# A Macaron block with 4-bit weights: the second wave's even planes on ScalarE, the first results' splits put off, ScalarE's casts at the ends of waves, and the opening's loads reordered

## The chip, the core and the metric

The kernel runs on one core of a Trainium2 chip. The core has a matrix engine (PE, TensorE), three engines for elementwise work (DVE is VectorE, ACT is ScalarE, POOL is GpSimd) and a sequencer that mostly issues transfers (SP). Each engine works through its own queue in order and waits at semaphores for the others. The metric is the device time of one execution in microseconds (us), as the median of several runs. The profile comes from one further execution, which has a time of its own.

## What is computed

The input is x of 2 x 1024 tokens with 1024 features. Three blocks follow each other, each on a layer-normalised copy of its input:

```
x = x + 0.5 * ffn(layernorm(x))
x = x + s4(layernorm(x))              # a convolution along the features
x = x + 0.5 * ffn(layernorm(x))
ffn(x) = (silu(x @ Wg) * (x @ Wu)) @ Wd
W[k, n] = s[k // 128, n] * (q4[k, n] - (z4[k // 128, n] + 1))
```

Wg and Wu are 1024 x 2752, Wd is 2752 x 1024. They come as 4-bit numbers, eight to a 32-bit word (the eight are eight consecutive rows k), with a scale and a zero point for each group of 128 rows. Both ffn blocks use the same weights.

## The kernel before

**Jobs.** The 2048 tokens are cut into four blocks of 512. Four blocks times two ffn passes make eight jobs, j = 0 to 7. Each job has an *up* stage (`gate_up`: the products with Wg and Wu, silu and the product of the two) and a *down* stage (`down`: the product with Wd). The change touches job 0 only, which is also the job in which the packed weights are first unpacked.

**The up stage.** The 43 column units (128 columns each of Wg or Wu, the last one shared by two half units) are taken in eight waves: waves 0 to 4 have six units (three of Wg, three of Wu), waves 5 and 6 have four, wave 7 has five. A wave holds one PSUM bank per unit and goes through the eight groups of 128 rows, g = 0 to 7. One wave and one g make a *step*: s = 8 * wave + g, 64 steps in all. In a step PE multiplies each unit's weights twice, once with the high part of the tokens (`xTh`, fp32r) and once with the low part (`xTl`, fp16), so a step of six units is twelve matmuls of line L842. After a unit's second matmul the bank is rescaled in place by the ratio of two groups' scales: even units by ACT (L800), odd ones mostly by DVE (L804), and PE may go on adding to that bank only afterwards. At g = 7 ACT makes the silu (L874) and DVE the product hf (L877) (`gated`), and POOL splits hf into a high and a low half for the down stage (hh, L879, and hl, L881).

**How a weight gets to PE.** For wave w:

- `fetch(w)` loads the packed words (L558) and `fetch_zeros(w)` the zero points (L565, from a table that the kernel wrote to DRAM itself).
- `split(w)` runs six DVE operations over them (`signed_bytes`): shift and mask for the even and for the odd nibbles (L619, x2), then for each of the two an addition of the zero points (L623) and an exclusive or that makes the byte a signed one (L625).
- `dequantize(w, j)`, j = 0 to 7, copies one of eight byte planes to int8 rows (L659, on POOL). Even j come from the even nibbles, odd j from the odd ones.
- `keep_bytes(w, odd)` writes the four even or the four odd planes to the DRAM tensor `wq` of the wave (L665, issued by SP).
- `load_bytes` reads 128 rows of `wq` for one step (`b<-wq`, L761, SP), and `make_weights` casts them to fp32r (`w_up`): on ACT (L775) where j = 0 and s > 2 and s % 8 is 1, 2 or 5, on POOL otherwise (L777). `next_weights` at step s loads for step s + 4 and casts for step s + 3. All of a step's rows hold even and odd planes, so none can be read before both writes have landed.

Wave 0 goes a shorter way in `start()`: `first_split` makes its bytes, with the even planes on ACT (L602, an addition of -128 on bytes that are still unsigned) and the odd ones on POOL (L600), each followed by a small transfer `b<-q` (L603, SP) of the first step's rows straight to the first byte tile. `keep_first` writes the rest to DRAM (L607). The layer norm of the first token block also runs there: `first_moments`, `first_rows` (normalised rows, L1793 on ACT, L1795 on DVE), and `first_turn(c)`, which transposes one block of 128 features on PE (L1808) and splits it into `xTh` and `xTl`: with ACT (L1810) and DVE (L1811), or for c = 3 and 5 with a copy by ACT (L1814) and the split on POOL (L1815, L1816). Block c is used from g = c on.

**What sets the order.** The program is written step by step; `at(up, s, f)` hangs a piece of other work before the products of step s, or at s + 0.5 between its two halves. `first_weights` gives the steps at which the splits, copies and writes of each wave are hung. A planner then orders each engine's instructions: by the order of writing among those that it holds to be ready, so that a later instruction can overtake an earlier one that it takes to be waiting. Where a piece is wrapped in `in_order_of_writing` or `pinned`, its instructions on the named engines keep the order of writing. DVE's splits and SP's loads are pinned in that way, and so is all of `start()`. The copies of L659, the casts on POOL and the splits of hf are not.

**Buffers.** hf has three buffers (`hfpool`), the cast weights five, the byte tiles six.

Of the kernel before, what the change touches and what calls it, by code (L numbers as in the profile page):

```python
# [32 lines left out]
GK = 8  # L33
# [24 lines left out]
def macaron_s4_kernel(  # L58
# [495 lines left out]
    def fetch(w, queues=(nc.sync, nc.sync)):  # L554

        raw = t4(f"raw_{w}").bitcast(I32)[:, : width_of(w)]
        for own, i, lo, hi in columns(w):
            queues[i].dma_start(raw[:, own], (gate_qw, up_qw)[i][:, lo:hi])  # L558
        packed[w] = [raw, None]
# [51 lines left out]
    def signed_bytes(key, raw, even, z):  # L611
# [9 lines left out]
        for part in (even, raw):  # L621
# [3 lines left out]
            nc.vector.tensor_scalar(both, both, 0x8080, None, ALU.bitwise_xor)  # L625
            yield

    def split(w):
        raw, z = packed[w]
        even = t4(f"even_{w}").bitcast(I32)[:, : width_of(w)]  # L630
        return signed_bytes(w, raw, even, z)
# [21 lines left out]
    def dequantize(w, j):  # L653
# [5 lines left out]
        nc.gpsimd.tensor_copy(unpacked[w][:, j % 2, j // 2, :], packed[w][j % 2][:, j // 2, :])  # L659
# [45 lines left out]
    def first_weights(up, dn, at):  # L705
# [3 lines left out]
        for w in range(1, len(WAVES)):  # L709
            s0 = (0, 4, 8 * w - 15)[min(w, 3) - 1]  # L710
            steps = (0.5, 1, 2, 2.5, 3, 3.5) if w == 1 else range(6)
            in_pieces(at, [(up, s0 + d) for d in steps], lambda w=w: split(w))
            copies = {1: (3.5,) * 8, 2: (3, 3, 4, 4, 6, 6, 7, 7)}.get(w, (3, 3, 4, 5, 6, 6, 7, 8))
# [5 lines left out]
            for odd, o in enumerate({1: (3.5, 3.5), 2: (5.5, 7.5)}.get(w, (6.5, 9.5))):  # L719
# [12 lines left out]
        for n in range(6 * 8):  # L732
            k, j = divmod(n, 8)
            a, rt = divmod(k, 3)
            if j == 0:
                at(*when(max(0, n - 7)), lambda a=a, rt=rt: fetch_down(a, rt))
                steps = [when(max(0, n - d)) for d in (4, 3, 3, 2, 1, 0)]
                if n == 16:
# [31 lines left out]
    def make_weights(i):  # L770
# [3 lines left out]
        if j == 0 and stage == "up" and s > 2 and s % GK in (1, 2, 5):  # L774
# [31 lines left out]
    def gate_up(j, b, hooks):  # L806
        hi, lo = pieces[b]
        ps = {}
        for s, (wi, g) in enumerate(STEPS):
            if j == 0 and s < 8:  # L810
# [61 lines left out]
    def gated(j, f, pg, pu):  # L872
# [6 lines left out]
        nc.gpsimd.tensor_copy(hi, hf)  # L879
        lo = hpool.tile([P, TB], F32R, tag="h", name=f"hl_{j}_{f}")  # L880
        nc.gpsimd.tensor_tensor(lo, hf, hi.bitcast(F32), ALU.subtract)  # L881
        h[f] = (hi, lo)

# [691 lines left out]
    def fast():  # L1575
# [5 lines left out]
        for j, (b, k) in enumerate(JOBS):  # L1581
# [88 lines left out]
            if j == 0:  # L1670
# [11 lines left out]
                steps = [(up, s) for s in range(17, 35, 2)]  # L1682
# [4 lines left out]
                for t in (0, 2):  # L1687
                    more = lambda t=t: first_rows(t, 512, HID)
                    at(up, 1, pinned(more, ET.DVE))
# [107 lines left out]
    def first_turn(c):  # L1797
# [11 lines left out]
        if c not in (3, 5):  # L1809
# [14 lines left out]
    def start():  # L1824
# [12 lines left out]
        for j in (1, 3):  # L1837
            dequantize_first(j)
        fetch(1)
        for j in (5, 7):  # L1840
            dequantize_first(j)
        first_scales = scales_in_pieces(0, 3, srow)
        mv, scratch = first_moments()
        next(first_scales)
        for j in (0, 2):
            dequantize_first(j)
# [5 lines left out]
        dequantize_first(4)  # L1852
# [115 lines left out]
```

## Time and profile before

| | |
|---|---|
| median of three runs | 2046.01 us (2045.63 to 2046.46) |
| the profiled execution's own time | 2046.72 us |
| its span, first to last instruction | 2044.9 us |
| PE busy | 2008.3 us (98%) |
| first matmul of L842 | 19.75 us |
| job 0's up stage, from there to the first matmul of L927 | 178.2 us |
| matmuls in it | 688 |
| a step of twelve matmuls with nothing in its way | 2.70 us |

Times within the trace are counted from the first instruction. A row of the timeline gives the start, the duration, the engine, the line, what is written and read with its shape, and how many like instructions were merged; the bracket gives the engine's idle time before it and what ended that. In a row that ends with "<-DMA b<-wq", the engine had nothing to do until that transfer had landed. A row of the windows gives the busy time of each engine within a stretch, then the mean TensorE clock (PEclk, 1.00 is full speed), the share of the transfer engines and GB/s. A busy PE can be a slow PE: the clock column tells.

### The profile page before, as it was taken

How to read it: one execution, taken by the hardware profiler on the slowest of the kernel's cores; microseconds unless marked ns; L12 is line 12 of the kernel's file. 1: busy time of each engine (PE TensorE's matmuls, PEld its weight loads, DVE VectorE, ACT ScalarE, POOL GpSimd, SP SyncE). 2: the span in 40 equal slices, each digit the busy share in tenths (PEclk: the TensorE clock that was granted, in tenths of full speed). 3: DMA queues.
4: the chain of work that ended last, by engine and by line, in shares of the span. 5: the costliest groups of instructions: out<-in, count | busy, mean ns of one | idle time of the engine just before them, and what ended most of it. 6: DMA issues, size and time to landing. Idle time of an engine off the chain costs nothing.

```text
span 2044.9 us, 29679 instructions
## 1 busy us (share of the span) xinstructions
PE 2008.3 (98%) x9202; PEld 1374.2 (67%) x9202; DVE 1628.9 (80%) x2712; ACT 1413.8 (69%) x2218; POOL 1369.2 (67%) x1772
## 2 busy tenths in 40 slices
PE   6999999999999999999999999999999999999998
PEld 4555776577766678665876578667686676866576
DVE  7887878867888787877778777887878878777776
ACT  6788787747675476777767777664776647767775
POOL 5877768757875478755976568754686636965542
PEclk9999999999999999999999999999999999999999
DMA  4334332233623327411462126333163331661113
GB/s 144 117 100 143 112 89 78 66 76 98 165 79 84 91 52 195 136 32 35 124 182 81 31 51 162 90 87 87 43 157 102 76 89 43 157 192 36 34 36 102
DMA packets 345965, 197.13 MB, mean 96 GB/s; under 512 B 166989, under 2 KB 323670, under 8 KB 345798
## 3 DMA queue, kind: packets, MB, share of 16 engines
q1 hardware_dynamic: 344382, 192.74, 34.7%
q10 hardware_dynamic: 1288, 2.01, 0.3%
q8 instruction: 75, 1.23, 0.2%
q14 instruction: 92, 0.75, 0.1%
q0 software_dynamic: 128, 0.39, 0.1%
HBM read 127.52 MB, written 48.57 MB: 86 GB/s over the span
## 4 chain that ended last, share of the span: by engine, by line
PE 91%; DVE 3%; POOL 2%; issue 1%; DMA 1%; ACT 1%; SPq 0%; DVEq 0%; POOLq 0%; ACTq 0%
PE pg L842 56%; PE po L927 30%; PE pc L1295 3%; PE pb L1295 1%; POOL q L659 1%; DVE pg L804 1%; DMA wq<-q 1%; ACT pg L800 0%; POOL w_up L777 0%; DVE po L804 0%; DVE rawd L623 0%; POOL hl L881 0%; DVE hf L877 0%; DVE rawd L619 0%; DMA b<-wq 0%
## 5 line engine op out<-in xcount | busy, mean ns | idle before, releaser
L800 ACT ACTIVATE pg<-pg,rat 128x512 f32<-128x512 f32 x1280 | 806.8, 660 | 391.3 <-PE pg L842 386.3
L804 DVE TENSOR_TENSOR pg<-pg,rat 128x512 f32<-128x512 f32 x1128 | 747.3, 691 | 154.1 <-PE pg L842 146.9
L842 PE MATMUL pg<-xTh,w_up 128*128 128x512 f32 x2752 | 848.0, 436 | 7.8 <-ACT pg L800 2.8
L842 PE MATMUL pg<-xTl,w_up 128*128 128x512 f16 x2752 | 711.3, 382 | 7.2 <-DVE pg L804 5.0
L842 PEld LDWEIGHTS pg<-xTh,w_up 128*128 128x128 f32 x2752 | 519.0, 189 | 173.8 <-ACT pg L800 9.4
L777 POOL CAST w_up<-b 128x768 fp32r<-128x768 int8 (+2 forms) x490 | 372.1, 765 | 365.5 <-PE pg L842 263.3
L800 ACT ACTIVATE po<-po,ratd 128x512 f32<-128x512 f32 x669 | 437.9, 662 | 144.0 <-PE po L927 143.4
L927 PE MATMUL po<-hl,w_down 128*128 128x512 f32 x1344 | 526.6, 394 | 2.0 <-DVE po L804 1.7
L927 PE MATMUL po<-hh,w_down 128*128 128x512 f32 x1344 | 521.3, 390 | 0.0
L804 DVE TENSOR_TENSOR po<-po,ratd 128x512 f32<-128x512 f32 x611 | 423.6, 695 | 112.3 <-PE po L927 111.8
L842 PEld LDWEIGHTS <-w_up 128*128 128x128 bf16 x2752 | 226.8, 98 | 345.3 <-issue 162.6
L777 POOL CAST w_down<-bd 128x512 fp32r<-128x512 int8 x352 | 217.6, 621 | 147.5 <-PE po L927 75.6
L927 PEld LDWEIGHTS po<-hl,w_down 128*128 128x128 f32 x1344 | 251.9, 188 | 65.1 <-DVE po L804 6.9
L927 PEld LDWEIGHTS po<-hh,w_down 128*128 128x128 f32 x1344 | 252.4, 188 | 50.6
L881 POOL TENSOR_TENSOR hl<-hf,hh 128x512 fp32r<-128x512 f32 x168 | 217.9, 1297 | 6.7
L879 POOL CAST hh<-hf 128x512 fp32r<-128x512 f32 x168 | 107.3, 639 | 81.9 <-DVE hf L877 63.1
L877 DVE SCALAR_TENSOR_TENSOR hf<-pg,rat,g 128x512 f32<-128x512 f32 x168 | 121.0, 746 | 45.5 <-ACT g L874 36.3
L874 ACT ACTIVATE g<-pg,rat 128x512 f32<-128x512 f32 x168 | 110.0, 687 | 33.9 <-PE pg L842 18.1
L980 POOL TENSOR_TENSOR x<-x,yr 128x512 f32<-128x512 f32 x52 | 66.8, 1284 | 0.0
L291 POOL TENSOR_TENSOR lo<-x,hi 128x512 f16<-128x512 f32 x48 | 61.9, 1291 | 0.0
L189 DVE BATCH_NORM_STATS2 stats<-x 128x6 f32<-128x512 f32 x88 | 59.9, 680 | 0.0
L289 POOL TENSOR_TENSOR mid<-hi,top 128x512 bf16<-128x512 f32 x48 | 55.9, 1165 | 0.0
(213 smaller groups left out, 1080.0 us busy)
## 6 DMA issues: line engine op xcount, KB each, us to landing
b<-wq SPq DMA_DIRECT2D x319, 96.0 KB
bd<-wdq SPq DMA_DIRECT2D x336, 64.0 KB
x<-in_L_attn_u_dram SPq DMA_DIRECT2D x30, 512.0 KB
yz<-y SPq DMA_DIRECT2D x56, 256.0 KB
yr<-yz SPq DMA_DIRECT2D x56, 256.0 KB
b<-wq SPq DMA_DIRECT2D x128, 64.0 KB
sz<-xn SPq DMA_DIRECT2D x16, 512.0 KB
st<-sz SPq DMA_DIRECT2D x64, 128.0 KB
```

Of the source, the lines that this page charges most:

```text
L291: nc.gpsimd.tensor_tensor(lo[:, own], n[:, own], hi[:, own].bitcast(F32), ALU.subtract)
L777: nc.gpsimd.tensor_copy(t, b)
L800: nc.scalar.activation(dst, src, AF.Copy, scale=sc)
L804: nc.vector.tensor_tensor(dst, src, sc.to_broadcast(list(dst.shape)), ALU.mult)
L842: product = lambda: nc.tensor.matmul(p, weights, (lo, hi)[k][:, g, :], start=(g == 0 and not done), stop=(g == GK - 1 and done), skip_grou ...
L874: nc.scalar.activation(g, pg, AF.Silu, scale=rat[:, 2 * f, GK - 1 :])
L877: nc.vector.scalar_tensor_tensor(hf, pu, last, g, ALU.mult, ALU.mult)
L879: nc.gpsimd.tensor_copy(hi, hf)
L881: nc.gpsimd.tensor_tensor(lo, hf, hi.bitcast(F32), ALU.subtract)
L927: nc.tensor.matmul(ps[c], w[:, bass.ts(c, P)], part, start=(f == 0 and k == 0), stop=(f == NF - 1), skip_group_check=True,)
L980: nc.gpsimd.tensor_tensor(part, part, rows_back.pop((a, t)), ALU.add)
L1295: nc.tensor.matmul(dst, lhsT, rhs, start=start, stop=stop, skip_group_check=True)
```

## The change

- `start()`: the two loads of wave 1's packed words (gate, up) are issued one by one, the first after the transfer of plane 5, the second after that of plane 2. Plane 7 and ACT's plane 0 are written ahead of or around the scales, and plane 6's transfer ahead of SP's 192 KB write of plane rows (`keep_first(0, 0)`).
- `first_rows(0, 512, 1024)` moves from DVE's work at step 1 into `start()`; block 7 of the tokens joins 3 and 5 in being split on POOL.
- Wave 1: the even planes are made by ACT with the addition of -128, as in wave 0, so that the exclusive or for the even nibbles falls away; the split then has five DVE operations, at steps 0.5, 1, 2.5, 3 and 3.
- Wave 2's copies of odd planes and the writes are hung half a step to a step earlier; the splits, copies and writes of waves 3 and 4 a step later.
- ACT's casts in job 0: none for s < 8; s % 8 in (5, 6, 7) for s = 8 to 23; (1, 2, 5) as before from s = 24 on. Counted out: ACT lost those of steps 5, 9, 10, 17 and 18 and got those of 14, 15, 22 and 23.
- The three splits of hf of wave 0 are written at the starts of steps 13, 14 and 15 instead of the end of step 7.
- The second split of the down weights (n == 8) is hung half a step earlier each; the down zero points (17, 19, ... 33) half a step later.

```diff
-    def fetch(w, queues=(nc.sync, nc.sync)):
+    def fetch(*what):
+        for _ in fetch_in_pieces(*what):
+            pass
+
+    def fetch_in_pieces(w, queues=(nc.sync, nc.sync)):
         raw = t4(f"raw_{w}").bitcast(I32)[:, : width_of(w)]
+        packed[w] = [raw, None]
         for own, i, lo, hi in columns(w):
             queues[i].dma_start(raw[:, own], (gate_qw, up_qw)[i][:, lo:hi])
-        packed[w] = [raw, None]
+            yield
...
-            nc.vector.tensor_scalar(both, both, 0x8080, None, ALU.bitwise_xor)
-            yield
+            if part is raw or even_signed:
+                nc.vector.tensor_scalar(both, both, 0x8080, None, ALU.bitwise_xor)
+                yield
...
-        return signed_bytes(w, raw, even, z)
+        return signed_bytes(w, raw, even, z, w > 1)
...
-        nc.gpsimd.tensor_copy(unpacked[w][:, j % 2, j // 2, :], packed[w][j % 2][:, j // 2, :])
+        q, src = unpacked[w][:, j % 2, j // 2, :], packed[w][j % 2][:, j // 2, :]
+        if w == 1 and j % 2 == 0:
+            nc.scalar.activation(q, src.bitcast(U8), AF.Identity, bias=minus_128)
+        else:
+            nc.gpsimd.tensor_copy(q, src)
...
-            s0 = (0, 4, 8 * w - 15)[min(w, 3) - 1]
-            steps = (0.5, 1, 2, 2.5, 3, 3.5) if w == 1 else range(6)
+            s0 = (0, 4, 8 * w - (14 if w < 5 else 15))[min(w, 3) - 1]
+            steps = (0.5, 1, 2.5, 3, 3) if w == 1 else range(6)
...
-            copies = {1: (3.5,) * 8, 2: (3, 3, 4, 4, 6, 6, 7, 7)}.get(w, (3, 3, 4, 5, 6, 6, 7, 8))
+            copies = {1: (3, 3, 3.5, 3.5) + (3.5,) * 4, 2: (3, 3, 4, 4, 5.5, 5.5, 6, 6)}
+            copies = copies.get(w, (3, 3, 4, 5, 6, 6, 7, 8))
...
-            for odd, o in enumerate({1: (3.5, 3.5), 2: (5.5, 7.5)}.get(w, (6.5, 9.5))):
+            for odd, o in enumerate({1: (3.5, 3.5), 2: (5.5, 7)}.get(w, (6.5, 9.5))):
...
                 steps = [when(max(0, n - d)) for d in (4, 3, 3, 2, 1, 0)]
+                if n == 8:
+                    steps = [(up, s0 + d) for d in (3.5, 4, 5, 5.5, 6.5, 7.5)]
...
-        if j == 0 and stage == "up" and s > 2 and s % GK in (1, 2, 5):
+        if j == 0 and stage == "up" and s % GK in ((), (5, 6, 7), (1, 2, 5))[(s > 7) + (s > 23)]:
             nc.scalar.copy(t, b)
...
         for s, (wi, g) in enumerate(STEPS):
+            if wi == 1 and g > 4 and put_off:
+                put_off.pop(0)()
...
-        nc.gpsimd.tensor_copy(hi, hf)
...
-        nc.gpsimd.tensor_tensor(lo, hf, hi.bitcast(F32), ALU.subtract)
         h[f] = (hi, lo)
+
+        def halves():
+            nc.gpsimd.tensor_copy(hi, hf)
+            nc.gpsimd.tensor_tensor(lo, hf, hi.bitcast(F32), ALU.subtract)
+
+        if j == 0 and f in WAVES[0]:
+            put_off.append(halves)
+        else:
+            halves()
...
-                steps = [(up, s) for s in range(17, 35, 2)]
+                steps = [(up, s + 0.5) for s in range(17, 35, 2)]
...
-                for t in (0, 2):
-                    more = lambda t=t: first_rows(t, 512, HID)
-                    at(up, 1, pinned(more, ET.DVE))
+                at(up, 1, pinned(lambda: first_rows(2, 512, HID), ET.DVE))
...
-        if c not in (3, 5):
+        if c not in (3, 5, 7):
...
-        for j in (1, 3):
+        second = fetch_in_pieces(1)
+        for j in (1, 3, 5):
             dequantize_first(j)
-        fetch(1)
-        for j in (5, 7):
-            dequantize_first(j)
+        next(second)
+        dequantize_first(7)
+        mv, scratch = first_moments()
+        dequantize_first(0)
         first_scales = scales_in_pieces(0, 3, srow)
-        mv, scratch = first_moments()
         next(first_scales)
-        for j in (0, 2):
-            dequantize_first(j)
+        dequantize_first(2)
+        next(second)
         next(first_scales)
...
         keep_first(1, 0, nc.gpsimd)
         dequantize_first(4)
+        dequantize_first(6)
         keep_first(0, 0, nc.sync)
-        dequantize_first(6)
...
-        for t in (1, 3):
+        for t in (0, 1, 3):
             first_rows(t, 512, HID)
```

## The prediction, made before the change was run

> **What bounds the kernel now.** I read the page's busy times and chain first, then the rows of each engine over the first 210 us, since all edits lie in job 0's up stage.
>
> ```profile
> PE 2008.3 (98%) x9202; PEld 1374.2 (67%) x9202; DVE 1628.9 (80%) x2712; ACT 1413.8 (69%) x2218; POOL 1369.2 (67%) x1772
> ...
> PE 91%; DVE 3%; POOL 2%; issue 1%; DMA 1%; ACT 1%; SPq 0%; DVEq 0%; POOLq 0%; ACTq 0%
> ```
>
> PE is the bound; only what lets it stand or slows its clock can be won. Counting L842's matmuls into steps, most take 2.70 us. The up stage takes 178.2 us where 688 matmuls at 0.2245 us (2.70 / 12) need 154.4: 23.8 us over, some 5 of it the transposes of tokens and scales, which stay. The rest has places, shown by PE's rows and by the rows that made it wait, in order of time:
>
> ```profile
> 16.02 0.49 SPq L603 DMA_DIRECT2D b<-q  x1
> 18.88 0.82 POOL L777 CAST w_up<-b 128x768 fp32r<-128x768 int8 x1 [2.15 <-DMA b<-q]
> 26.63 2.08 DVE L1795 TENSOR_SCALAR xn<-x,mv,r 128x512 f32<-128x512 f32 x2
> 29.84 0.59 PE L842 MATMUL pg<-xTl,w_up 128*128 128x512 f16 x2 [1.22 <-DVE pg L804]
> 49.42 1.56 ACT L775 CAST w_up<-b 128x768 fp32r<-128x768 int8 x2 [2.29 <-DMA b<-wq]
> 50.89 1.84 ACT L874 ACTIVATE g<-pg,rat 128x512 f32<-128x512 f32 x3
> 51.62 0.38 PE L842 MATMUL pg<-xTl,w_up 128*128 128x512 f16 x1 [1.41 <-ACT g L874]
> 72.31 0.83 ACT L775 CAST w_up<-b 128x768 fp32r<-128x768 int8 x1 [3.84 <-DMA b<-wq]
> 73.05 0.65 ACT L800 ACTIVATE pg<-pg,rat 128x512 f32<-128x512 f32 x1
> 73.75 0.73 PE L842 MATMUL pg<-xTh,w_up 128*128 128x512 f32 x2 [2.60 <-ACT pg L800]
> 184.66 0.59 PE L842 MATMUL pg<-xTl,w_up 128*128 128x512 f16 x2 [1.25 <-DVE pg L804]
> ```
>
> Twice ACT stood at a cast whose bytes had not landed, with silus or rescales behind it in its queue; PE, far from needing those casts (they are made three steps ahead), stood for the rescales. The later stall costs more than its 2.60 us, by the windows:
>
> ```profile
> 72.00:75.00 3.00, 1.25 (x5) 0.61 (x6) 0.24 (x1) 2.69 (x5) 2.92 (x6) 1.00 0.75 225
> 75.00:78.50 3.50, 3.44 (x9) 1.91 (x8) 2.42 (x4) 2.88 (x6) 3.42 (x6) 0.53 0.91 272
> ```
>
> After it PE ran at PEclk 0.53: step 15 took 4.41 us, 1.71 over. Why the bytes were late is in the rows of POOL and SP:
>
> ```profile
> 57.38 1.56 POOL L881 TENSOR_TENSOR hl<-hf,hh 128x512 fp32r<-128x512 f32 x1
> 61.76 2.32 POOL L659 COPY q<-raw 128x768 int8<-128x768 int8 x2
> 66.75 0.55 SPq L665 DMA_DIRECT2D wq<-q  x1
> 69.79 1.78 SPq L761 DMA_DIRECT2D b<-wq  x4
> ```
>
> DVE had the odd nibbles of wave 2 ready at 56.7; POOL, busy with wave 0's splits (three of 0.61 + 1.56 to 1.99), copied them until 66.7.
>
> **The change, part by part.** *Opening.* The first matmul waits for plane 6's transfer, issued at 16.02 though ACT had made the plane at 15.04: SP was writing 192 KB from 15.35. Now that write comes behind; on ACT 0.46 us of waiting for the scales goes too. SP's queue ahead of it becomes seven transfers of about 0.6 us and two loads of 0.42 to 0.58 from 9.8 on: issue at about 15.3. 0.7 us won; ends 0.3 and 1.4 (landing faster than 2.80 us without the write ahead of it). The later loads of wave 1 cost nothing: DVE uses the words at 24.97. `first_rows(0)` fills DVE's idle 1.60 us before 21.68 and leaves one of the two operations at 26.63, 1.04 us, in front of the rescales that PE waited 1.22 us for: 1.0 won (0 to 1.2).
>
> *ACT's even planes.* The nearest row is ACT's own in the opening, 128x768 int8 from uint8 in 0.92 each, four in 3.41 us. POOL loses four copies (0.82 to 1.16), DVE one exclusive or (0.73). ACT's load in steps 3 to 5 is then 3.4 + 1.9 + 2.5 + 1.9 (rescales) + 1.8 (three token blocks) + 0.2 = 11.7 us in the 10.4 us that these steps took. Its queue behind a plane holds rescales, and PE waits for these. Rescales of a step's first half have a slack of 1.3 us, so not all shows: cost 1.0; ends 0 (step 5's cast, 0.83, is gone as well) and 2.0.
>
> *Block 7 on POOL*: 0.62 + 1.33 to 1.97 on POOL, 0.69 off DVE, ACT alike. Its copy is made at 41.2 and PE asks for the low half at step 7, 46.35. Hidden if POOL takes it before the casts that wait for wave 1's bytes: 0.2; ends 0 and the rival below.
>
> *Wave 1's bytes and step 8.* The odd planes can follow DVE's exclusive or some 3 us earlier, and only four copies stand before the odd write instead of eight: `wq` lands about 42 instead of 46.7, and step 8's cast ends near 45.5, before PE wants it. The casts of 9 and 10, now POOL's, may wait there: behind them stand wave 2's even planes, which nobody needs for 20 us. Step 8 was 1.78 over: 1.6 won (0.8 to 1.8). Steps 10 and 11 waited 0.62 + 0.18 for DVE, whose operations beside POOL's splits lasted 1.00 instead of 0.54 us; the splits leave, and wave 3's start moves off step 9: 0.6 (0 to 0.8).
>
> *Wave 2's bytes and steps 14, 15.* Without 6.9 us of splits ahead of it, POOL's odd planes end near 56, the write lands near 59, the bytes near 61; step 17's cast is asked for at about 65. And it is POOL's now, which holds no rescale. 2.60 + 1.71 = 4.3 won. Here a rule speaks against the larger sum: the Trainium skill, TensorE: Matmul & The Clock Gate, section Why this matters for your kernels, has the clock halve after gaps of more than about 3 us, a whole window of idle. By that, 2.60 us would not have slowed PE and only 2.6 is won. The row has 0.53 right behind the stall, with 1.9 us of idle in the 3.4 us before; I take the row, 4.3 (2.6 to 4.5).
>
> *The splits put off.* POOL gets three times 1.9 to 2.6 us plus the casts of 17 and 18 in steps 13 to 15, beside wave 3's even planes. From step 13 to 20 that makes, at 1.9: splits 5.7, wave 1's own splits 5.7, five casts 4.2, eight planes 6.6, scales 1.8 = 24 us in 19.4. But POOL is free from about 56 to 62 and the splits are ready, so the planner can put some there; wave 1's splits can wait. What must be in time: wave 3's odd planes by about step 20. ACT's casts at 21 to 23 relieve POOL. hf has three buffers, so wave 1's last hf waits for the last split put off. Cost 0.5; ends 0 and the rival.
>
> *Half-step moves.* DVE's zero points came together with a split at steps 18, 26 and 34, where PE stood 0.22 + 0.25 + 0.58: 0.6 (0 to 1.0). At step 57 two shifts and an addition of 1.77 us stood before the rescales; one shift now goes into DVE's idle 1.43 us before hf: 0.9 (0 to 1.4). Waves 3 and 4 a step later: covered, as before wave 3's planes were done at 79.6, 22 us before use; no cost beyond the case above. SP's loads for them move along, with words there over 10 us ahead.
>
> **Sum.** Won 0.7 + 1.0 + 1.6 + 0.6 + 4.3 + 0.6 + 0.9 = 9.7; lost 1.0 + 0.2 + 0.5 = 1.7; net 8.0. The profiled execution took 2046.72 (span 2044.9 and 1.8 around it), so 2038.7; it lay 0.7 above the median, so 2046.0 - 8.0 = 2038.0. Behind job 0 PE runs almost without gaps and is only shifted.
>
> **Rivals.** *All hides*: losses nothing, each gain at its upper end, 12.1: 2034. For it: ACT's cast of step 5 and its stalls go. Against: 11.7 us into 10.4. *Block 7 waits*: its split is written behind the cast for step 8. If POOL keeps that order it comes after wave 1's bytes, at 45.3 + 2.6 = 47.9, PE wants it at about 45.4: 2.5, and 1.7 for a halved clock: 2042.2. Against: before, scale operations written later (46.24) overtook that cast (48.72). *POOL runs short, mildly*: wave 3's odd planes come 3 us after step 20, ACT stands at step 25's cast as it did at 17's, clock included: 4.7 more, 2042.7. *Slower: POOL runs short in full.* Written order kept at steps 13 to 20 and the longest durations (splits 2.6, planes 0.95, scales 1.8): the cast for step 19 ends 24.5 us after step 13 begins, wanted after 16.7: 7.8 late, 1.7 of clock, 1.5 for hf's buffers, 3.8 if wave 2's odd planes are still in the queue: 14.8, less the 0.5 counted: 2052.3. It decides from 12.1 us on. For it: 24 us into 19.4; against: the free time before step 13.
>
> **Chances.** Forecast 0.65 (2035.5 to 2041); all hides 0.13; block 7 0.10; POOL mildly 0.08; in full 0.04. A measurement of this kernel can tell about 0.2%, 4.1 us, from no change: faster is below 2041.9, slower above 2050.1. The first two are faster, of the next two a third: 0.83; same 0.13; slower 0.04. The range 2033.5 to 2042.8 leaves out the slower case and the outer halves of the mild ones.
>
> **What would show it.** Right: first matmul near 19.0; no ACT row with "<-DMA b<-wq" over 1 us; steps 8, 14 and 15 near 2.7 (14 with 0.5 of transposes); PEclk 1.00 around 75; job 0's up stage near 171 us (178.2 - 8.0 + 0.7, as the start counts apart). Wrong: PE waiting on ACT's rescales in steps 4 to 6 for over 2 us, on xTl at step 7, or on w_up or a cast between steps 17 and 25. The forecast falls if the planner's order elsewhere in the eight jobs shifts as well.

## The result and the profile after

The changed kernel takes 2039.13 us in the median (2038.68 to 2040.46, 8 runs) against 2046.08 us (2044.44 to 2047.63, 8 runs) of the kernel before in the same session: a ratio of 0.9966, 95% interval 0.9956 to 0.9977, or 6.95 us less. The forecast was 2038.0. Its profiled execution has a span of 2036.9 us against 2044.9. Lines have moved: the matmuls of the up stage are L857 (before L842), ACT's and DVE's rescales L813 and L817, the casts L788 (ACT) and L790 (POOL), ACT's new planes L667, POOL's planes L669, the writes to `wq` L675, hf L892 and its split L898 and L899. Waves and steps count from 0, as ahead of the prediction; where a text on record names a wave by a word ("third wave"), it counts from one, and the "third wave's bytes" in the texts on c1 and c3, which bear on step 21, are wave 3's.

The page's busy times and its chain, as shown of before:

```profile
PE 2005.1 (98%) x9202; PEld 1373.4 (67%) x9202; DVE 1627.9 (80%) x2710; ACT 1416.2 (70%) x2221; POOL 1372.1 (67%) x1771
...
PE 93%; DVE 3%; ACT 2%; issue 1%; POOL 1%; DMA 1%; SPq 0%; ACTq 0%; DVEq 0%; POOLq 0%
```

PE's busy time fell by 3.2 us, though its work is the same: 1.7 of that is the stretch at half clock at 75 us, which is gone. The rest of the 8.0 us is standing time. POOL's share of the chain fell from 2% to 1%, ACT's rose from 1% to 2%.

The rows that answer to those of before, in order of time (engines mixed):

```profile
14.90 1.13 SPq L608 DMA_DIRECT2D b<-q  x2
18.31 0.82 POOL L790 CAST w_up<-b 128x768 fp32r<-128x768 int8 x1 [1.70 <-DMA b<-q]
26.35 1.65 DVE L1817 TENSOR_SCALAR xn<-x,mv,r 128x512 f32<-128x512 f32 x1
29.12 0.59 PE L857 MATMUL pg<-xTl,w_up 128*128 128x512 f16 x2 [1.17 <-DVE pg L817]
54.77 3.46 POOL L669 COPY q<-raw 128x768 int8<-128x768 int8 x4
61.30 2.32 SPq L774 DMA_DIRECT2D b<-wq  x5
71.21 0.75 DVE L429 RECIPROCAL safe<-safe 128x96 f32<-128x96 f32 x1 [1.71 <-POOL safe L427]
73.54 1.15 PE L857 MATMUL pg<-xTh,w_up 128*128 128x512 f32 x3 [0.91 <-DVE hf L892]
88.98 0.83 ACT L788 CAST w_up<-b 128x768 fp32r<-128x768 int8 x1 [2.19 <-PE pg L857]
90.42 0.95 PE L857 MATMUL pg<-xTl,w_up 128*128 128x512 f16 x3 [1.53 <-ACT pg L813]
```

Wave 2's odd planes end at 58.2 (before 66.7), their write is issued at 58.26 and the bytes are asked for at 61.30 (before 69.79): the stall of 2.60 us at step 14 is gone. New are two waits: 0.91 us in step 16, where PE wants a bank that hf still holds, and DVE stood 1.71 for POOL's part of the second scales; and 1.53 us in step 21, where ACT stood at a cast. The bracket of that cast names PE; but SP asked for wave 3's bytes only at 86.48, after the last plane at 83.49, and in a3 and in c1 to c3 below the same cast's bracket names the transfer (c2: `[2.22 <-DMA b<-wq]`), so it is the bytes that it waited for. The windows around 75 us:

```profile
72.00:75.00 3.00, 2.10 (x9) 0.91 (x8) 2.84 (x5) 1.82 (x3) 3.00 (x6) 1.00 0.07 25
75.00:78.50 3.50, 3.50 (x18) 2.08 (x16) 3.25 (x6) 3.16 (x6) 3.50 (x5) 1.00 0.25 91
```

PEclk is 1.00 in both; before it was 0.53 in the second. Instead of nine matmuls PE does eighteen in the same 3.5 us, and POOL is busy without a gap.

Counted from step to step, before less after, the job's up stage and its start have this balance:

| place | before | after | won |
|---|---|---|---|
| start of step 0 | 19.75 | 19.19 | 0.57 |
| step 2 | 4.97 | 4.90 | 0.07 |
| steps 3 to 6 (ACT's even planes, step 5's cast gone) | 13.14 | 13.22 | -0.1 |
| steps 7 and 8, less step 9 | 3.25, 4.47, 2.73 | 2.83, 2.70, 3.00 | 1.9 |
| steps 10 and 11 | 3.53, 3.08 | 2.84, 2.70 | 1.1 |
| steps 14 and 15 | 5.81, 4.41 | 2.71, 2.70 | 4.8 |
| step 16 | 2.70 | 4.06 | -1.36 |
| steps 21, 22, 23 | 2.70, 2.70, 2.72 | 4.40, 2.83, 3.07 | -2.2 |
| steps 18, 26, 34 | 3.07, 2.95, 3.43 | 2.71, 2.71, 2.82 | 1.2 |
| step 57, less 58 and 59 | 3.99, 2.27, 2.25 | 2.80, 2.58, 2.80 | 0.3 |

In sum 6.4; the first matmul of the down stage (L951) comes 6.38 earlier, at 191.60. By the last job's down stage the lead is 7.20: another 0.8 is won on the way, 0.3 of it in the first matmuls of job 0's down stage and 0.3 near 875 us, in job 3's up stage, where before waits for a rescale and after does not. No edit was aimed at these places. The last 0.8 of the span's 8.0 come in the tail behind the last down stage's start, which took 88.7 to 89.8 us in the fourteen profiles, of kernels that do not differ there. The medians, 6.95 apart, fit the 7.2.

### The profile page after: what moved, and what is told of

Its sections match the earlier page's. It is cut to its first block, busy times and chain, and to the rows that moved or that the text cites. A ratio compares the mean times of both kernels' runs of the same rounds, so it can differ in the third digit from the quotient of the medians.

```text
span 2036.9 us, 29679 instructions
## 1 busy us (share of the span) xinstructions
PE 2005.1 (98%) x9202; PEld 1373.4 (67%) x9202; DVE 1627.9 (80%) x2710; ACT 1416.2 (70%) x2221; POOL 1372.1 (67%) x1771
## 4 chain that ended last, share of the span: by engine, by line
PE 93%; DVE 3%; ACT 2%; issue 1%; POOL 1%; DMA 1%; SPq 0%; ACTq 0%; DVEq 0%; POOLq 0%
PE pg L857 57%; PE po L951 30%; PE pc L1319 3%; PE pb L1319 1%; ACT pg L813 1%; DVE pg L817 1%; DVE po L817 0%; DVE rawd L628 0%; POOL w_up L790 0%; DMA x<-in_L_attn_u_dram 0%; DVE hf L892 0%; POOL hl L899 0%; DMA b<-wq 0%; POOL hh L898 0%; PE pt L239 0%
## 5 line engine op out<-in xcount | busy, mean ns | idle before, releaser
L813 ACT ACTIVATE pg<-pg,rat 128x512 f32<-128x512 f32 x1280 | 807.0, 661 | 387.1 <-PE pg L857 383.2
L817 DVE TENSOR_TENSOR pg<-pg,rat 128x512 f32<-128x512 f32 x1128 | 747.8, 692 | 150.7 <-PE pg L857 143.8
L857 PE MATMUL pg<-xTh,w_up 128*128 128x512 f32 x2752 | 845.5, 435 | 6.3 <-DVE pg L817 2.5
L857 PE MATMUL pg<-xTl,w_up 128*128 128x512 f16 x2752 | 708.9, 382 | 4.8 <-DVE pg L817 2.4
L857 PEld LDWEIGHTS pg<-xTh,w_up 128*128 128x128 f32 x2752 | 518.7, 189 | 170.4 <-ACT pg L813 6.9
L790 POOL CAST w_up<-b 128x768 fp32r<-128x768 int8 (+2 forms) x491 | 375.3, 770 | 362.5 <-PE pg L857 259.1
L813 ACT ACTIVATE po<-po,ratd 128x512 f32<-128x512 f32 x669 | 437.9, 662 | 143.3 <-PE po L951 142.7
L951 PE MATMUL po<-hl,w_down 128*128 128x512 f32 x1344 | 526.6, 393 | 1.6 <-DVE po L817 1.4
L951 PE MATMUL po<-hh,w_down 128*128 128x512 f32 x1344 | 521.3, 390 | 0.0
L817 DVE TENSOR_TENSOR po<-po,ratd 128x512 f32<-128x512 f32 x611 | 423.7, 696 | 112.8 <-PE po L951 112.3
L857 PEld LDWEIGHTS <-w_up 128*128 128x128 bf16 x2752 | 226.9, 98 | 342.8 <-issue 158.4
L790 POOL CAST w_down<-bd 128x512 fp32r<-128x512 int8 x352 | 219.0, 625 | 145.0 <-PE po L951 71.9
L951 PEld LDWEIGHTS po<-hl,w_down 128*128 128x128 f32 x1344 | 251.9, 188 | 64.5 <-DVE po L817 6.1
L951 PEld LDWEIGHTS po<-hh,w_down 128*128 128x128 f32 x1344 | 252.4, 188 | 50.6
L899 POOL TENSOR_TENSOR hl<-hf,hh 128x512 fp32r<-128x512 f32 x168 | 218.5, 1300 | 6.5
L898 POOL CAST hh<-hf 128x512 fp32r<-128x512 f32 x168 | 107.3, 639 | 81.4 <-DVE hf L892 62.6
L892 DVE SCALAR_TENSOR_TENSOR hf<-pg,rat,g 128x512 f32<-128x512 f32 x168 | 121.0, 746 | 40.5 <-ACT g L889 34.7
```

What stands on the lines that cost most here:

```text
L790: nc.gpsimd.tensor_copy(t, b)
L813: nc.scalar.activation(dst, src, AF.Copy, scale=sc)
L817: nc.vector.tensor_tensor(dst, src, sc.to_broadcast(list(dst.shape)), ALU.mult)
L857: product = lambda: nc.tensor.matmul(p, weights, (lo, hi)[k][:, g, :], start=(g == 0 and not done), stop=(g == GK - 1 and done), skip_grou ...
L892: nc.vector.scalar_tensor_tensor(hf, pu, last, g, ALU.mult, ALU.mult)
L951: nc.tensor.matmul(ps[c], w[:, bass.ts(c, P)], part, start=(f == 0 and k == 0), stop=(f == NF - 1), skip_group_check=True,)
```

## The experiments

All ratios are to the kernel before, whose medians in the three sessions lay at 2046.38 (a), 2046.06 (b) and 2046.21 (c and d); differences to after are between medians of different sessions, which these three show to be good to some 0.3. A kernel's profile names the same lines as after's, except where said.

### Which part carries the gain

**a1: the kernel before, with ACT's casts at the new steps and nothing else.**

```diff
-        if j == 0 and stage == "up" and s > 2 and s % GK in (1, 2, 5):
+        if j == 0 and stage == "up" and s % GK in ((), (5, 6, 7), (1, 2, 5))[(s > 7) + (s > 23)]:
```

> The kernel before with only the steps changed at which ACT casts in job 0 (none below step 8, then 5, 6, 7 of each eight up to step 23). First theory, a cast in ACT's queue that waits for late bytes is what stopped PE, and the late bytes themselves would not: the stalls of 1.41 us at step 8 and 2.60 us at step 14 and the halved clock behind the second go, 5.5 us in all, so about 2040.5, though step 17's bytes still land at about 72. Rival, the late bytes are the cause: the wait only moves from ACT's rescales to the cast that PE itself needs, the clock halves all the same, about 2045.

Measured: 2046.48 (2044.46 to 2048.11), ratio 1.0001 (0.9992 to 1.001). The theory that the casts' place alone wins fell. The waits moved to where POOL now makes the cast, and to the scales (a row of PE and one of DVE; the lines are those of before):

```profile
64.90 0.82 PE L842 MATMUL pg<-xTl,w_up 128*128 128x512 f16 x3 [1.92 <-POOL w_up L777]
78.73 0.75 DVE L429 RECIPROCAL safe<-safe 128x96 f32<-128x96 f32 x1 [4.09 <-POOL safe L427]
```

With the bytes as late as before, taking the cast off ACT only changes the name of the engine that waits for them (at 51.02 as well, 1.03 us). POOL's backlog then reaches the second scales, PE stands 2.33 for hf behind them, step 16 takes 6.11 us, and a window at half clock (3.41 us, see the last section) follows at 81.11.

**a2: after, with wave 0's splits at the end of step 7 again.**

```diff
-        if j == 0 and f in WAVES[0]:
+        if False:
             put_off.append(halves)
```

> The changed kernel with wave 0's splits of hf back at the end of step 7. First theory, the splits put off are what makes POOL short after step 13 (PE's new waits of 1.36 us in step 16 and 1.71 us in step 21): both go; wave 2's bytes land some 5 us later, at about 66, which is still before PE reaches step 16 at 71, so nothing comes in their place: about 2036. Rival, putting off is what brought wave 2's bytes in time: ACT or PE waits for them again at steps 13 to 16, the clock with it, 2042 or more.

Measured: 2044.34 (2042.33 to 2045.54), ratio 0.9991 (0.9984 to 0.9998): 5.2 above after. POOL makes the splits among wave 2's even planes, so that the odd ones come at 61.13 to 64.99 instead of 54.77 to 58.23; the rows of POOL and PE:

```profile
61.13 3.86 POOL L669 COPY q<-raw 128x768 int8<-128x768 int8 x4
69.98 0.83 POOL L790 CAST w_up<-b 128x768 fp32r<-128x768 int8 x1 [4.99 <-PE pg L857]
78.85 1.65 PE L857 MATMUL pg<-xTh,w_up 128*128 128x512 f32 x3 [4.75 <-DVE hf L892]
```

POOL then stands 4.99 us at its first cast of wave 2, until the bytes asked for at 67.96 have landed (this bracket names PE, but in b4 below the same cast's reads `[5.05 <-DMA b<-wq]`); the scales are behind that cast, DVE stands 5.79 at their reciprocal with hf behind it, and PE 4.75. Two windows at half clock follow. Steps 14 and 15, where the kernel before lost its 4.8, take 2.7 each here as well: with the cast moved to POOL the late bytes no longer stop PE there, but at step 16, which takes 8.99. So the put-off splits are worth more than any other part that was taken back by itself; the half-step moves and the new order of the opening were not, and their sizes are read from the traces alone.

**a3: after, with ACT's casts at the old steps** (a1's edit the other way round).

> The changed kernel with ACT's casts back at 1, 2 and 5 of each eight. First theory: step 17's bytes now land at about 63, before its cast comes up at 65.7, so step 14 stays free; step 9's cast comes up at about 43 with the bytes at 45.3, ACT stands some 2 us and PE with it in steps 6 to 8: about 2 us more than the changed kernel, 2041. Rival, the places of the casts carried the whole gain: both stalls come back, 2044 or more. A third outcome, that the places don't matter once the bytes are early: 2039.

Measured: 2039.97 (2038.94 to 2040.82), ratio 0.9969 (0.9957 to 0.998). Only 0.8 above after: once the bytes are early, it matters little which engine casts. Step 3 grew by 0.5 (ACT's cast of step 5 is back and stands 1.92 for its transfer), step 21 shrank by 1.2.

**a4: after, with wave 1's even planes on POOL again** (with their exclusive or and the old steps).

```diff
-        return signed_bytes(w, raw, even, z, w > 1)
+        return signed_bytes(w, raw, even, z)
...
-        if w == 1 and j % 2 == 0:
+        if False:
...
-            steps = (0.5, 1, 2.5, 3, 3) if w == 1 else range(6)
+            steps = (0.5, 1, 2, 2.5, 3, 3.5) if w == 1 else range(6)
...
-            copies = {1: (3, 3, 3.5, 3.5) + (3.5,) * 4, 2: (3, 3, 4, 4, 5.5, 5.5, 6, 6)}
+            copies = {1: (3.5,) * 8, 2: (3, 3, 4, 4, 5.5, 5.5, 6, 6)}
```

> The changed kernel with wave 1's even planes back on POOL, with the exclusive or for them and the old steps. First theory, ACT's planes were worth little to PE, since the casts moved away: step 8's weights come some 3 us later, at about 48.7, where PE wants them at 48.2: 0.5 to 1 us lost, ACT's delays in steps 3 to 5 (0.2) gone: about 2039.5. Rival, the even planes carry the gain at step 8: 2041 or more.

Measured: 2042.14 (2041.0 to 2043.63), ratio 0.998 (0.9971 to 0.9988): 3.0 above after. The price shows first at block 7, which the change also gave to POOL (a row of PE):

```profile
46.07 0.81 PE L857 MATMUL pg<-xTl,w_up 128*128 128x512 f16 x3 [1.38 <-POOL xTl L1838]
```

This is the rival "block 7 waits" of the prediction. It did not come in the kernel after because four planes had left POOL: block 7 on POOL needs the planes on ACT. Whether the planes need block 7's move as well was not tried.

### Where the new waits at steps 16 and 21 come from

**b1: ACT's casts at the ends of wave 3's steps too.**

```diff
-... ((), (5, 6, 7), (1, 2, 5))[(s > 7) + (s > 23)]:
+... ((), (5, 6, 7), (1, 2, 5))[(s > 7) + (s > 31)]:
```

> The changed kernel with ACT's casts at 5, 6, 7 for the eight steps of wave 3 too, so that those of steps 25 and 26 are POOL's. First theory: PE's wait of 1.53 us in step 21 is ACT's cast of step 25 standing for wave 3's bytes (read from 86.5 on) with rescales behind it; on POOL nobody waits behind it: step 21 back to 2.7 us, the 0.5 us over in steps 22 and 23 mostly too, about 2037.3. Rival, as the casts moved alone showed, the wait only goes to the next one that the bytes hold up (POOL's cast of step 24, at 88.5, is needed by PE at about 94): nothing won, or the scales' way below: 2039.

Measured: 2038.96 (2037.78 to 2040.69), ratio 0.9963 (0.9948 to 0.9977), not to be told from after. Steps 21 to 23 take 2.7 each, 2.2 less, and the wait comes back one wave on, at the first bytes of wave 4 that ACT casts, where PE stands 0.68 in step 29; steps 29 to 31 take 1.4 more than in after. The row of ACT:

```profile
110.56 0.83 ACT L788 CAST w_up<-b 128x768 fp32r<-128x768 int8 x1 [1.85 <-DMA b<-wq]
```

**b2: after, with the second scales hung from step 18 instead of 14.**

```diff
-                for first_use, s, k0, k1 in ((5, 1, 3, 9), (14, 6, 9, 15), (30, 11, 15, WIDE)):
+                for first_use, s, k0, k1 in ((5, 1, 3, 9), (18, 6, 9, 15), (30, 11, 15, WIDE)):
```

> The changed kernel with the second group of scales made at steps 18 to 19.5 instead of 14 to 15.5 (they are first used at step 24). First theory: PE's wait of 1.36 us in step 16 is DVE's reciprocal of these scales, which waited 1.71 us for POOL and stood before wave 1's hf in DVE's queue, so it goes: 2037.8. Rival, it is the last hf waiting for one of its three buffers, held by the split put off: the wait stays, 2039. A third outcome: the scales collide with the wait at step 21 instead and nothing is won in sum.

Measured: 2040.2 (2039.0 to 2041.54), ratio 0.9971 (0.996 to 0.9982). Step 16 is free (2.70), so its wait was the scales and not hf's three buffers. But step 20 takes 5.88 (rows of DVE and PE):

```profile
83.74 0.75 DVE L429 RECIPROCAL safe<-safe 128x96 f32<-128x96 f32 x1 [3.23 <-POOL safe L427]
85.56 0.59 PE L857 MATMUL pg<-xTl,w_up 128*128 128x512 f16 x2 [3.04 <-DVE pg L817]
```

These scales belong to units that PE reaches at step 24. Nobody needs them at step 20; they stop PE because DVE takes its queue in order and the rescales stand behind a reciprocal that waits for POOL.

**b4: a2 and b2 together** (splits at once, scales from step 18).

> The changed kernel with wave 0's splits at the end of step 7 (the run that lost 5.2 us) and the second scales at steps 18 to 19.5. First theory: what that run lost was not the late bytes as such but the scales behind a POOL cast that waits for them: DVE waited 5.79 us for the scales with hf's behind, and the clock halved. With the scales out of the way PE meets the bytes in time: most of it comes back, 2037 to 2039. Rival, the bytes are too late for PE itself: step 16's cast ended at 70.8 and later ones follow: 2042 or more.

Measured: 2045.14 (2043.44 to 2046.4), ratio 0.9994 (0.9985 to 1.0003). Step 16 is free, step 20 takes 9.60: `[5.20 <-DVE pg L817]` and a window at half clock behind it. The stop moves with the scales, so in a2, too, it is their wait for POOL that brings POOL's lateness to PE; nothing is won by it, as the scales wait here as well.

**c1: after, with the guard of the second scales on DVE.** The three operations in front of the reciprocal leave POOL (later lines are one further on).

```diff
-        nc.gpsimd.tensor_tensor(safe, flat(s), flat(s), ALU.mult)
-        nc.gpsimd.tensor_scalar(safe, safe, 2.0**-60, None, ALU.is_lt)
-        nc.gpsimd.tensor_tensor(safe, safe, flat(s), ALU.add)
+        guard = nc.vector if k0 == 9 else nc.gpsimd
+        guard.tensor_tensor(safe, flat(s), flat(s), ALU.mult)
+        guard.tensor_scalar(safe, safe, 2.0**-60, None, ALU.is_lt)
+        guard.tensor_tensor(safe, safe, flat(s), ALU.add)
```

> The kernel after, with the three short operations in front of the second scales' reciprocal (the square, the comparison, the sum) on DVE in place of POOL, where they stood behind casts and splits. Theory (the 0.91 us that PE stands in step 16, and the 3.04 in step 20 when the scales' steps came later, are the scales waiting their turn on a POOL that is short of time between steps 13 and 21): step 16 falls from 4.06 us to at most 3.0, nothing comes back at step 20, and since POOL is also relieved of some 2 us the wait at step 21 gets shorter; the job's end comes 1.4 to 2.5 us earlier, 2036.6 to 2037.8. Rival (whatever leaves step 16 is met again at step 21, where ScalarE waits for the third wave's bytes, because that point hangs on POOL's planes alone): step 16 falls and step 21 grows by as much, 2038.7 to 2039.6. Third outcome: DVE itself gets late with the sums, step 14 or 15 grows, 2039.5 to 2041.

Measured: 2039.07 (2037.94 to 2040.33, 7 runs), ratio 0.9965 (0.9954 to 0.9977). In the trace the theory holds: the three operations take 0.87, 0.50 and 0.79 us on DVE, where it had stood 1.71 in after, the reciprocal no longer waits for POOL, step 16 takes 2.69, step 21 takes 3.15 in place of 4.40, and step 15 3.65 in place of 2.70.

The first matmul of the down stage (L952 here) starts 2.0 us earlier than in after. Of this 0.8 is left at the end of the trace, which is of the fastest of the seven runs, and the medians show none: the expected 2036.6 to 2037.8 missed. The median lies in the rival's 2038.7 to 2039.6, though step 21 did not grow, as the rival had it. Of the other 1.2, 0.4 go in the first matmuls of the down stage, where PE waits 0.28 at 194.48 for a rescale, and 0.3 near 874 us in job 3's up stage, where c1 and c2 wait as before does and after does not; the rest is spread from there to the last job.

**d1: after, with waves 3 and 4 started one step earlier again,** as the kernel before had them.

```diff
-            s0 = (0, 4, 8 * w - (14 if w < 5 else 15))[min(w, 3) - 1]
+            s0 = (0, 4, 8 * w - 15)[min(w, 3) - 1]
```

> The kernel after, with the splits of the fourth and fifth waves (and their planes and stores) started one step earlier, where the kernel before had them. Theory (POOL is short of time between steps 13 and 21, whatever the steps say): the planes come into the program earlier but POOL gets to them no sooner than its casts let it, so the wait at step 21 changes by less than 0.7 us, while DVE's split stands a step nearer to the first results and step 12 or 13 grows: 2038.8 to 2040.5. Rival (the step that the change gave away is itself what makes the fourth wave's bytes late at step 21): the 1.7 us at step 21 go and the time falls to 2037 to 2038.

Measured: 2038.78 (2037.26 to 2039.04, 5 runs), ratio 0.9961 (0.9947 to 0.9975). The theory said that POOL would get to the planes no sooner; that fell. Wave 3's last odd planes, first POOL's rows of after, then the row of d1:

```profile
79.43 1.17 POOL L669 COPY q<-raw 128x768 int8<-128x768 int8 x1
80.56 1.27 POOL L899 TENSOR_TENSOR hl<-hf,hh 128x512 fp32r<-128x512 f32 x1
81.78 0.94 POOL L898 CAST hh<-hf 128x512 fp32r<-128x512 f32 x1
82.66 0.83 POOL L669 COPY q<-raw 128x768 int8<-128x768 int8 x1
```

```profile
75.80 1.61 POOL L669 COPY q<-raw 128x768 int8<-128x768 int8 x2
```

Hung a step earlier, all four planes go ahead of wave 1's own splits, which nobody needs before the down stage, and end at 77.4 instead of 83.5. Step 21 takes 2.69. What it costs is spread: steps 9 and 10 grow by 0.14 and 0.34, as wave 3's split meets DVE's rescales there, step 16 by 0.37 and step 20 by 0.27. From step 10 to L951 the trace is 1.3 us shorter than after's, but its opening had two windows at half clock and step 10 begins 0.7 later. The medians (2038.78 and 2039.13) can't be told apart: the rival was right on step 21, and its 2037 to 2038 did not come.

### Where the opening's gain goes

**b3: after, with the rows of the third token tile prepared in `start()`** instead of in step 1.

```diff
-                at(up, 1, pinned(lambda: first_rows(2, 512, HID), ET.DVE))
...
-        for t in (0, 1, 3):
+        for t in (0, 1, 2, 3):
             first_rows(t, 512, HID)
```

> The changed kernel with the last of DVE's half rows of normalised tokens (t = 2) made in the opening as well, in DVE's idle 1.53 us before 21.8. First theory: the wait of 1.17 us at step 2 stayed because this operation, 0.54 us by itself, took 1.65 beside POOL's split of a token block; away from there it goes: 1 us less, 2038.1. Rival, the wait is PE's own pace (the rescale can't come sooner, since its matmul ended just before) or something else is next: under 0.3 us, 2039.

Measured: 2039.75 (2038.84 to 2042.31), ratio 0.9969 (0.9956 to 0.9981). Step 2 takes 3.58 instead of 4.90: without that `xn` the wait at 29.12 goes. But the operation's own 1.65 us were not the cause, as rows of DVE, POOL and PE in b1 show, where it is still in its place:

```profile
25.61 0.53 DVE L1817 TENSOR_SCALAR xn<-x,mv,r 128x512 f32<-128x512 f32 x1
25.82 1.45 POOL L1838 TENSOR_TENSOR xTl<-turn,xTh 128x512 f16<-128x512 f32 x1
26.06 1.62 DVE L624 TENSOR_SCALAR raw<-raw 128x768 int32<-128x768 int32 x1
28.35 0.59 PE L857 MATMUL pg<-xTl,w_up 128*128 128x512 f16 x2 [1.22 <-DVE pg L817]
```

There `xn` took 0.53, the shift behind it met POOL's L1838 and took 1.62 instead of 0.55, and PE waited as in after. It is so in a2, a4, b4 and c1 too; in after, a3 and b2 `xn` met L1838. In b3 the shift runs from 25.83 to 26.38, the same POOL operation from 26.05, and the shift takes 0.55; in d1, where POOL comes later, `xn` is in its place, both are through before L1838, and step 2 takes 3.58 as well.

In the end nothing is won, since step 9 takes 4.46 instead of 3.00. Rows of SP, ACT and PE in b3, just after SP has issued wave 3's fetch from 45.36 to 47.58:

```profile
46.29 1.29 SPq L570 DMA_DIRECT2D z<-z_dram  x2
47.63 1.99 SPq L774 DMA_DIRECT2D b<-wq  x4
52.77 0.83 ACT L788 CAST w_up<-b 128x768 fp32r<-128x768 int8 x1 [2.18 <-PE pg L857]
54.22 0.95 PE L857 MATMUL pg<-xTl,w_up 128*128 128x512 f16 x3 [1.46 <-ACT pg L813]
```

Step 10 began at 54.23 in after, 54.60 in a3, 54.30 in b1, 54.44 in b2 and 54.22 in b3 (53.88 in c1), though step 2 had begun at 26.75 to 27.79. ACT's cast for step 13 waits for bytes that are queued on SP behind the fetch of wave 3. The bracket in b3 names PE, that of the same cast in c1 the transfer:

```profile
52.43 0.83 ACT L789 CAST w_up<-b 128x768 fp32r<-128x768 int8 x1 [1.02 <-DMA b<-wq]
```

In b4 the planner put two rescales ahead of this cast; it stood until 53.40 for the same transfer, but step 9 took 2.69 and step 10 began at 53.49.

**c2: b3, and wave 3's fetch hung three steps later,** behind the loads of three more tiles of bytes.

```diff
-                at(up, s0 + (3 if w == 2 else 6), lambda both=both: in_order_of_writing(both, ET.SP))
+                at(up, s0 + 6, lambda both=both: in_order_of_writing(both, ET.SP))
```

> The kernel after, with the fourth wave's raw words and zero points fetched three steps later, behind the loads of three more tiles of bytes in the queue of SP, and the rows of the third token tile prepared ahead of the main loop instead of in step 1. Theory (step 10 began at 54.2 to 54.4 us in five kernels whatever the opening had won, because ScalarE's cast for step 13 waits for bytes that are queued behind that fetch): with the rows ahead step 2 takes 3.6 in place of 4.9 as before, and now step 9 does not grow, so step 10 begins near 52.5 to 53.2 and the whole ends 1 to 1.5 us earlier, 2037.5 to 2038.3. Rival (what holds step 10 is not the place in the queue but when the second wave's bytes are made and stored at all): step 10 begins at 54.2 to 54.4 again and the time is 2039 to 2040. Third outcome: the fetch comes too late for DVE's split at step 10, a new wait at steps 11 to 14, 2040 or more.

Measured: 2038.19 (2036.92 to 2040.55, 5 runs), ratio 0.9965 (0.9951 to 0.9979). With four loads of bytes at 43.67 ahead of the fetch, the rows of SP and ACT:

```profile
43.67 1.77 SPq L774 DMA_DIRECT2D b<-wq  x4
45.53 0.38 SPq L563 DMA_DIRECT2D raw<-_L_ffn_gate_qweight_dram  x1
...
49.53 0.85 ACT L788 CAST w_up<-b 128x768 fp32r<-128x768 int8 x1
```

The cast has no wait ahead of it, step 9 takes 2.71, step 10 begins at 51.51, and L951 comes 2.7 earlier than in after. Step 0 ran at full clock in this execution and is 1.35 shorter; but b3, whose step 0 was as short (4.34), reached L951 only at 191.68, 2.8 behind c2, so that the place of the fetch decides whether such a gain is kept. At the end of the trace, of the fastest of the five runs, 1.9 is left against after. The fetch alone, without the rows, was not tried.

**c3: c1 and c2 together.**

> Both edits together: the second scales' guard on DVE, the fourth wave's fetch behind the bytes, the third token tile's rows ahead. If both theories hold the gains add, since one lies ahead of step 10 and the other behind step 13: 2035 to 2037. If POOL's shortage up to step 21 sets the third wave's bytes on a clock of its own, what is won ahead of step 10 is met again as a longer wait at step 21, and the sum is no better than the better of the two: 2037.5 to 2039.5.

Measured: 2036.54 (2035.87 to 2038.58, 4 runs), ratio 0.9955 (0.9938 to 0.9971). All four runs lie below the fastest of after's eight; by the medians it is 2.6 below after and 9.7 below before, the best version of the study, though the intervals of the two ratios to before still overlap. From step 10 to the down stage (L952 here) it takes 136.1 us where c2 takes 137.4 and after 137.4. The wait at step 21 stayed (`[1.41 <-ACT pg L814]`): c1's relief there did not show here, its 1.5 at step 16 did. Step 10 began at 52.74, with the opening at half clock as in after, so 1.5 is won ahead of it. d1's and b1's edits on top of it were not tried.

## Why the prediction was right, and which of its steps were not

The mechanism of the largest gains was right, but the net (8.0 forecast, 6.95 by the medians, 7.2 in the trace ahead of the tail) lies nearer than its terms, which in part is luck. In the up stage the gains came to 10.0 (9.7 forecast) with single terms off by up to 0.9, and the losses to 3.6 (1.7 forecast), so that 6.4 were won there; the other 0.8 of the 7.2 came behind it, from no term of the sum.

- *Wave 2's bytes, steps 14 and 15*: forecast 4.3, measured 4.8. The row, not the rule, gave the size: the kernel before lost the clock behind a wait of 2.60, and both parts came back. Two edits free these steps, each without the other: with the splits at once (a2) and with the old casts (a3) step 14 takes 2.7. But "it is POOL's now, which holds no rescale" was no protection: in a1 and a2 POOL, standing at its cast, held the scales, DVE the rescales and hf behind them, and PE paid at step 16. The put-off splits carry the gain because they make the bytes early for every engine.
- *Wave 1's bytes and step 8*: forecast 1.6, measured 1.9 with step 9. *Steps 10 and 11*: 0.6 forecast, 1.1 measured; d1 shows that 0.34 of it, and 0.14 in step 9, come from moving wave 3's start off step 9.
- *First matmul*: 0.7 forecast, 0.57 measured. But step 9 took back about half of it (3.00 instead of 2.70), and b3 shows that more would have been lost whole: the bytes for step 13 come through SP's queue at a time of their own, which c2 moved. The sum added gains ahead of step 9 as if nothing fixed in time stood behind them; this is the step that the prediction lacked. The 1.0 at step 2 would have gone the same way.
- *Step 2*, forecast 1.0, measured 0.07. "One of the two operations ... leaves" was true, "1.04 us" each was not: the one left took 1.65, beside POOL's L1838, and PE waited 1.17, nearly as before. Half of a pair's time (0.67 and 1.50 us, the second beside POOL) was taken for the time of one; and where the one left is short, the shift behind it is long (b1). What costs is that one of DVE's operations meets L1838.
- *ACT's even planes*, cost 1.0 forecast, 0.1 measured over steps 3 to 6, where step 5's cast is gone at the same time; against a4, with the planes on POOL, steps 3 to 5 take 0.3 more. The planes took 0.88 each, in two pairs (33.36 and 36.17), with a pair of rescales in between, and these met the slack that the prediction named and used only in part.
- *The splits put off, and POOL behind step 13*: cost 0.5 forecast, 3.5 measured (1.36 at step 16, 2.2 at steps 21 to 23). The rival "POOL runs short, mildly" described it: ACT standing at step 25's cast, without the half clock. Two steps failed. "Waves 3 and 4 a step later: covered ... 22 us before use" counted to PE's use; but ACT casts three steps ahead and in order. In after it reaches that cast 9.5 us before step 24 begins (86.8 and 96.3), and from the last plane to the cast it took 5.5 (83.49 to 88.98), so the planes are due 15 us before use; and d1 frees step 21 by undoing this alone. And the scales were counted as 1.8 us of POOL's load, not as a thing that DVE waits for with rescales behind it (b2, c1).
- *Half-step moves*: 0.6 forecast and 1.2 measured at steps 18, 26 and 34; 0.9 forecast and 0.3 measured at step 57, of whose 1.19 steps 58 and 59 took back 0.86, where DVE's next operations now stand (177.24, 0.89 us; 179.25, 1.25 us). The shift did not go into DVE's idle 1.43 us, which stand in after too, but behind the first hf (173.31). By the diff the moves there are not half a step each: the second operation moved a whole step and the third not at all.
- *Rivals*: "all hides" fell by the 3.5; "block 7 waits" did not come, but a4 shows it at 1.38 us once POOL has four more planes; "in full" did not come either; how POOL's lateness reaches the clock is seen in a2.

What stays open: why 0.8 to 1.2 us of what c1 and c2 won in job 0's up stage were lost again behind it. The places of some of it are known (c1), the cause is not.

## What to carry to other kernels

Gains of single stalls add up only as far as nothing later hangs on a time of its own; ask of each what is late next, and look for a step that begins at the same time in several versions. In an engine that works in order, an operation is due when the engine reaches it, not when its result is used: measure the slack of a transfer to the first instruction that waits for it, and keep operations that wait for another engine's backlog out of the queue that carries the sums. Work on an overfull engine that nobody needs soon belongs behind what others wait for: putting off three splits was worth 5.2 us, more than the changes of who casts (0.8) and who copies (3.0).

## What the runs showed of the chip

**The clock.** Over job 0 it changes in these traces only at the ends of windows of 3.413 us (before's two, at 20.63 and 75.24, lie 16 of them apart, a1's two, at 19.67 and 81.11, 18), and then stays at 0.50 for a whole window. What it goes with is how long PE was busy in the window before, not how long one wait was. First the windows of before at the stall of 2.60 us, then those of b2, whose wait was longer, 3.04 us, but divided between two windows; the first figure behind the comma is PE's busy time, the third from the end PEclk:

```profile
71.83:75.24 3.41, 1.43 (x6) 0.64 (x7) 0.48 (x1) 2.93 (x6) 3.29 (x6) 1.00 0.73 215
75.24:78.65 3.41, 3.41 (x8) 2.03 (x8) 2.22 (x4) 2.79 (x5) 3.33 (x6) 0.50 0.93 281
```

```profile
80.92:84.33 3.41, 1.60 (x8) 0.65 (x7) 0.59 (x1) 1.72 (x3) 2.62 (x6) 1.00 0.33 115
84.33:87.75 3.42, 2.19 (x10) 1.44 (x10) 3.31 (x7) 1.33 (x3) 1.37 (x2) 1.00 0.63 167
```

Of before's 3.41 us PE was busy 1.43, and the next window ran at 0.50; of b2's it was busy 1.60, and the clock stayed. In the first 230 us of the fourteen profiles, each of the four windows with PE busy under 1.5 us was followed by one at half clock, of thirteen with 1.5 to 1.81 us eight were, and above that none, but for two that were at half clock themselves. So the rule of the Trainium skill that the prediction weighed (TensorE: Matmul & The Clock Gate, section Why this matters for your kernels) holds here with a smaller gap than it says: about half a window idle was enough in twelve of these seventeen. What decides between 1.5 and 1.81 us these figures do not show: in the opening PE was busy 1.61 us in after's window and 1.81 in d1's, and step 0 was slow, 1.79 in c2's, and it was not. Where the windows lie differs from profile to profile, and step 0 took 5.5 to 5.8 us with such a window (7.02 with two), 4.3 without, in profiles of kernels with the same opening.

**DVE beside POOL.** In after, DVE's normalisation of 128x512 f32 (L1817) took 0.54 us at 19.75 and 1.65 us at 26.35, when POOL ran a two-operand instruction of that size (L1838, from 26.43 to 27.71). In b1 the shift of 128x768 int32 (L624) took 1.62 us beside it, and 0.55 in after without it. DVE's rescales of PSUM banks (L817) were hardly touched: four took 2.69 us in b3, from 26.30, beside the same POOL instruction (L1837 there, 26.05 to 27.51), and 2.52 in after, from 28.39, without it.
